# An adaLN + attention + mixture-of-experts layer on one core: second sequence's rows multiplied in the warm-up, three modulation sums in one PSUM bank, partial logits transposed and summed on VectorE

## The chip, the cores and the metric

One Trainium2 chip, and of it one core. The core has TensorE (PE, matrix products; its weight loads are listed apart as PEld), VectorE (DVE), ScalarE (ACT), GpSimd (POOL) and SyncE (SP, which starts most transfers). All work on tiles of up to 128 partitions in on-chip memory; products land in PSUM, in banks of 128 x 512 floats. The metric is the device time of one execution in microseconds, and a verdict compares medians.

## The reference

Everything is float32. Two sequences (B = 2) of 1024 rows with D = 512 go through an adaLN block: attention of a simple kind, then a mixture of eight experts with two chosen per row, and a shared expert.

```
mod = (_silu(L0_c) @ L0_wmod).reshape(B, 6, 1, -1)
sa, ca, ga, sb, cb, gb = mod[:, 0] ... mod[:, 5]
ga, gb = (2 * (g >= 0) - 1) * max(|g|, 0.25)     for g in ga, gb
h = _layernorm(x) * (1 + ca) + sa
Xn = _layernorm(h, gamma, beta)
Q, K, V = split(Xn @ W_in + b_in);  K, V rotated in their first 256 columns
A = 0.5 * sum over rows (cos_sim(K) * cos_sim(V)) + 0.5
x = x + ga * ((A * Q) @ W_out + b_out + h)
h = _layernorm(x) * (1 + cb) + sb
scores = softmax(h @ gate_w);  the 2 best of 8 experts by row
x = x + gb * (sum of w_e * expert_e(h) + shared(h))
```

A depends on all rows of a sequence, so a sequence's K and V come before any of its outputs.

## The kernel before, in words

The 2048 rows are 16 tiles of 128 rows, in four groups of four; tiles 0 to 7 are the first sequence. The program is one instruction stream written out by hand; a scheduler of the tile framework then orders each engine's instructions by what they wait for and by the order in the code. So an instruction that is taken out can change the order of its neighbours. The order inside an engine's queue is fixed when the kernel is built, and an instruction waits for all ahead of it.

*Modulation.* `silu(c)` is turned into a padded operand `sc_pad` of 32 columns for each quarter k of the 512 inputs. `mod_parts` (L235) multiplies, for one of the six parts m, four quarters of the weights side by side: `tile_position=(0, k * CT)` puts quarter k in columns 32k (CT = 32), so four partial sums lie at partitions 0, 32, 64 and 96 of one bank (L240), and ScalarE copies them out (L248). Two forms then add the four partial sums. `spread_now` (L283) multiplies by a selector, `pick`, broadcast to 128 columns: the result has a modulation row copied into all 128 partitions, ready for elementwise use, and ScalarE adds 1 or 0 while copying (L289). `mod_sum` (L250) multiplies by `pick` with its two columns, which gives the two sequences' rows in partitions 0 and 1; `mod_add` adds a constant and stores the row to `mods` in memory, and `mod_gate` forms the clipped gate. The rows are later read back from `mods` into all partitions (`spread`, in `before_mix`), and `turn_mod` transposes two of them on TensorE.

*Start.* `turn_over(n, row)` (L213) multiplies a matrix of ones n times; nobody reads the result. It fills TensorE while data come in: three such products at the start, four after the rows of the first sequence (`ca1[0]`, `sa[0]`). Meanwhile VectorE and ScalarE normalize tiles 0 and 1 (`norm1_in`, `norm1_mid`, `norm1_out`: two layer norms; the outcome is `hn`), and `turn1` transposes a tile (`tr_a`, L330) and lets ScalarE scale it into `xnT` (L377).

*The loop over tiles 0 to 7 of the first sequence.* For tile t: normalize tile t+2, multiply K (`kv_half(t, 0)`: four 128x512 products, L394), transpose tile t+1, do what the table `side` has for t, multiply V (`kv_half(t, 1)`), and accumulate A (`kv_back`). `side` holds the modulation work that isn't needed at once: the second sequence's rows at t = 0, products for ga, cb, sb and gb from t = 1 on, their sums a tile later. Products take turns in three PSUM banks (`mm_ps`), transpositions in others (`tr_ps`).

*The loop over the first sequence's second part, with the second sequence's K and V between.* For tile t: `project` (L555), `norm2` (layer norm again; `hr`), `turn2` (transposition `tr_c`, scaled into `hT` at L586). The table `plan` puts in the second sequence's `kv_half`, `turn1` and `norm1`, the shared expert's chunks (L824, with the sigmoid at L797), and, for each group of four tiles, the routing: `logit_parts` (L624) multiplies four quarters of `gate_w` side by side like the modulation, which leaves partial logits `lgp`, transposed, at partitions 32k + e of a 128 x 512 tile. `route` (L636) multiplies each of the four 128-column pieces by `pick_e`, a 0/1 matrix of 8 columns that sums over k, which also transposes: rows become partitions. VectorE copies the 128 x 32 logits out and goes on with softmax (ScalarE, L654), the two best (L664 and on) and counts; `place_rows` (L689, L692) ranks the rows among those of the same expert, and GpSimd scatters them to `hbuf`. ScalarE loads a table of constants whenever the kind of function changes (square root, exponential, sigmoid).

*After that* the second sequence is projected, the last two groups are routed, and the expert blocks of 128 rows follow (L1416, L1428, L1444, from about 330 us to 640 us), with weights streaming in, and at the end the shared expert's remaining parts and the sums.

Of the kernel before, what the change touches and what calls it, by code (L numbers as in the profile page):

```python
# [8 lines left out]
FP = mybir.dt.float32  # L9
# [3 lines left out]
ALU = mybir.AluOpType  # L13
AX = mybir.AxisListType
# [4 lines left out]
P = 128  # L19
# [5 lines left out]
def kernel(  # L25
# [20 lines left out]
    nc = tc.nc  # L46
    B, S, D = x.shape
    E, _, H = w_gate.shape
    KC = D // P
    CT = P // KC  # L50
# [29 lines left out]
    const = ctx.enter_context(tc.tile_pool(name="const", bufs=1))  # L80
# [16 lines left out]
    def mm_ps(name):  # L97
        return ps_mm.tile([P, 512], FP, tag="mm", name=name)

    def tr_ps(name):  # L100
        return ps_tr.tile([P, 512], FP, tag="tr", name=name)
# [9 lines left out]
    ident = const.tile([P, P], FP, name="ident")  # L111
# [3 lines left out]
    ones_t = const.tile([P, P], FP, name="ones_t")  # L115
# [39 lines left out]
    def load_mod(m, home):  # L155
        t = act_tile(home, f"wmod{m}")
        nc.sync.dma_start(t, wm[:, :, m * D : (m + 1) * D])
        return t
# [32 lines left out]
    wm_ga = load_mod(2, 3)  # L191
# [4 lines left out]
    wm_cb = load_mod(4, 4)  # L196
    wm_sb = load_mod(3, 5)
# [6 lines left out]
    wm_gb = load_mod(5, 0)  # L204
# [5 lines left out]
    def turn_over(n, row):  # L210
        ps = tr_ps(f"turn_over_{n}")
        for _ in range(n):
            nc.tensor.matmul(ps, ones_t, row, start=True, stop=True)  # L213
# [8 lines left out]
    silu = nc.vector.tensor_mul(sc_pad[:, :, 0:B], csb, sig_c)  # L222
    pick = late.tile([P, B], FP, name="pick")
    with tc.issue_after(silu.ins):
        nc.vector.tensor_reduce(
            pick, ident.rearrange("p (k c) -> p c k", k=KC)[:, 0:B, :], AX.X, ALU.add
        )
    pick_e = const.tile([P, E], FP, name="pick_e")
    with tc.issue_after(silu.ins):
        nc.vector.tensor_reduce(  # L230
            pick_e, ident.rearrange("p (k c) -> p c k", k=KC)[:, 0:E, :], AX.X, ALU.add
        )
    parts = {}

    copied = []  # L235
# [11 lines left out]
            )  # L247
        copied.append(nc.scalar.copy(t, ps))  # L248

    def mod_sum(m, w):  # L250
        ps = mm_ps(f"modsum_{m}")
        nc.tensor.matmul(ps[:B, :], pick, w[:, 0, :], start=True, stop=True)
        return ps[:B, :]


    def mod_add(m, w, plus):
        t = w[:B, 1, :]
        nc.vector.tensor_scalar(t, mod_sum(m, w), plus, None, ALU.add)
        nc.sync.dma_start(mods[m], t)
        return t  # L260

    def mod_gate(m, w):

        ps = mod_sum(m, w)
        t, mag = w[:B, 1, :], w[:B, 2, :]
        nc.vector.tensor_scalar(t, ps, 0.0, 2.0, ALU.is_ge, ALU.mult)
        nc.scalar.activation(mag, ps, AF.Abs)
        nc.vector.tensor_scalar(mag, mag, 0.25, None, ALU.max)
        nc.vector.scalar_tensor_tensor(t, t, 1.0, mag, ALU.subtract, ALU.mult)
        nc.sync.dma_start(mods[m], t)  # L270
# [9 lines left out]
        mod_parts(m, w, t)  # L280
        return t

    def spread_now(t, b, plus, tag):  # L283
        ps = mm_ps(f"{tag}_{b}")
        nc.tensor.matmul(
            ps, pick[:, b : b + 1].to_broadcast([P, P]), t, start=True, stop=True
        )
        row = late.tile([P, D], FP, tag=tag, bufs=B, name=f"{tag}_{b}")
        nc.scalar.activation(row, ps, AF.Identity, bias=plus)  # L289
        return row  # L290

    modT = late.tile([P, 2, KC, B], FP, name="modT")

    def turn_mod(i, raw):
        ps = tr_ps(f"modT_{i}")
        for f in range(KC):
            nc.tensor.transpose(
                ps[:, f * B : (f + 1) * B], raw[:, f * P : (f + 1) * P], ident[0:B, 0:B]
            )
        nc.vector.tensor_copy(modT[:, i].rearrange("p f b -> p (f b)"), ps[:, 0 : KC * B])  # L300

    ca1, sa, ga, cb1, sb, gb, cg, sg = ([None] * B for _ in range(8))
    zero_t = const.tile([P, 1], FP, name="zero_t")
# [23 lines left out]
    def transposes(src, name):  # L327
        ps = tr_ps(f"tr_{name}")
        for f in range(KC):
            nc.tensor.transpose(  # L330
                ps[:, f * P : (f + 1) * P], src[:, f * P : (f + 1) * P], ident
            )
        return ps
# [4 lines left out]
    if NS != 4 or B != 2:  # L338
        raise ValueError("the homes are laid out for two sequences of two groups")

    hn_of = {}

    h_of = {}

# [14 lines left out]
    def norm1_out(t):  # L359
        h, b = h_of.pop(t), t // NJ  # L360
        nc.vector.scalar_tensor_tensor(h, h, rs1[:, t : t + 1], sa[b], ALU.mult, ALU.add)
        hn_of[t] = ln.tile([P, D], FP, tag="hn", name=f"hn_{t}")
        normalize(hn_of[t], h, f"b{t}")
# [6 lines left out]
    def turn1(t):  # L370
        g, j = t // 4, t % 4
        hn = hn_of.pop(t)
        if j == 0:
            xnT[g] = act_tile(XNT_HOME[g], f"xnT_{g}")
        ps = transposes(hn, f"a{t}")
        for f in range(KC):
            nc.scalar.activation(  # L377
                xnT[g][:, f, j * P : (j + 1) * P],
                ps[:, f * P : (f + 1) * P],
                AF.Identity,  # L380
                bias=colsb[:, 1, f : f + 1],
                scale=colsb[:, 0, f : f + 1],
            )
# [219 lines left out]
    rows = const.tile([P, NT, TOPK], I32, name="rows")  # L603
# [32 lines left out]
    def route(g, lgp):  # L636

        t0 = g * 4
        ps = tr_ps(f"lg_{g}")
        for j in range(4):  # L640
            nc.tensor.matmul(
                ps[:, j * E : (j + 1) * E],
                lgp[:, j * P : (j + 1) * P],
                pick_e,
                start=True,
                stop=True,
            )
        lg = small.tile([P, 4, E], FP, tag="lg", name=f"lgs_{g}")
        nc.vector.tensor_copy(lg.rearrange("p j e -> p (j e)"), ps[:, 0 : 4 * E])
        mx = small.tile([P, 4], FP, tag="mx", name=f"mx_{g}")  # L650
        nc.vector.tensor_reduce(mx, lg, AX.X, ALU.max)
        nc.vector.tensor_sub(lg, lg, mx.unsqueeze(2).to_broadcast([P, 4, E]))
        ex = small.tile([P, 4, E], FP, tag="ex", name=f"ex_{g}")
        nc.scalar.activation(ex, lg, AF.Exp)  # L654
        sm = small.tile([P, 4], FP, tag="sm", name=f"sm_{g}")
        nc.vector.tensor_reduce(sm, ex, AX.X, ALU.add)
        nc.vector.reciprocal(sm, sm)
        p = small.tile([P, 4, E], FP, tag="p", name=f"p_{g}")
        nc.vector.tensor_mul(p, ex, sm.unsqueeze(2).to_broadcast([P, 4, E]))

        top = small.tile([P, 4, 8], FP, tag="top", name=f"top_{g}")
        place = small.tile([P, 4, 8], U32, tag="place", name=f"place_{g}")
        for j in range(4):
            nc.vector.max(top[:, j, :], p[:, j, :])  # L664
            nc.vector.max_index(place[:, j, :], top[:, j, :], p[:, j, :])
        nc.vector.tensor_copy(wts[:, t0 : t0 + 4, :], top[:, :, 0:TOPK])
        no = small.tile([P, 4, TOPK], FP, tag="no", name=f"no_{g}")
        nc.vector.tensor_copy(no, place[:, :, 0:TOPK])
        pick = picks[:, t0 : t0 + 4]
        for s in range(TOPK):  # L670
            nc.vector.tensor_tensor(
                pick[:, :, s, :],
                no[:, :, s : s + 1].to_broadcast([P, 4, E]),
                ex_no.unsqueeze(1).to_broadcast([P, 4, E]),
                ALU.is_equal,
            )
        both = small.tile([P, 4, E], FP, tag="both", name=f"both_{g}")
        nc.vector.tensor_add(both, pick[:, :, 0, :], pick[:, :, 1, :])
        for j in range(4):
            nc.vector.tensor_add(seen[:, t0 + j + 1, :], seen[:, t0 + j, :], both[:, j, :])  # L680
        return both
# [363 lines left out]
        return kvp.tile([P, D + 2 * R2], FP, tag="acc", bufs=1, name=f"acc_{b}")  # L1045

    def second_rows():
        ca1[1] = spread_now(parts_ca, 1, ones_t[:, 0:1], "ca1")
        sa[1] = spread_now(parts_sa, 1, zero_t, "sa")

    def own(m, w):
        mod_parts(m, w, w[:, 0, :])

    raws = {}

    def add(m, w, plus):
        raws[m] = mod_add(m, w, plus)


    side = {  # L1060
        0: [second_rows],
        1: [lambda: own(2, wm_ga)],
        2: [lambda: mod_gate(2, wm_ga), turn_wq],
        3: [lambda: own(4, wm_cb), lambda: own(3, wm_sb)],
        4: [lambda: add(4, wm_cb, 1.0), lambda: add(3, wm_sb, 0.0)],
        5: [lambda: own(5, wm_gb), lambda: turn_mod(0, raws[4])],
        6: [lambda: mod_gate(5, wm_gb), lambda: turn_mod(1, raws[3])],
        7: [lambda: before_mix(0)],
    }
    turn_over(3, ones_row)  # L1070
    parts_ca = own_parts(1, wm_ca)
# [4 lines left out]
    parts_sa = own_parts(0, wm_sa)  # L1076
    norm1_mid(0)
    sa[0] = spread_now(parts_sa, 0, zero_t, "sa")
    turn_over(4, parts_sa)
    norm1_in(2)  # L1080
    norm1_out(0)
    norm1_mid(1)
    turn1(0)
    norm1_out(1)
    acc = start_acc(0)
    for t in range(NJ):
# [472 lines left out]
    sums = list(range(NT))  # L1559
# [106 lines left out]
```

## Time and profile before

| what | value |
|---|---|
| three runs | 776.17, 777.97 and 780.13 us, median 777.97 |
| profiled execution, its own time | 776.02 us |
| its span, first to last instruction | 774.1 us |
| mean granted TensorE clock | 0.997 of full speed |
| records of the 128x8 logit products (L641) | 32, 256 ns in the median |
| records of the 128x512 modulation sums (L252) | 8, 592 ns in the median |
| records of the side-by-side products (L240) | 48, 592 ns in the median |

The profile names a group of instructions by line, engine, operation and tiles, output first. The matmul records are pipelined: the duration of one (592 ns) is longer than the step from one to the next (about 430 ns), so slots are read from the start of one piece of work to the start of the next. A float32 product leaves two records. "[1.04 <-ACT hn L325]" says that the engine was idle 1.04 us and that the instruction of ScalarE at L325, writing hn, ended that. ScalarE's timeline around one such place:

```profile
173.93 1.28 ACT L316 ACT_TABLE_LOAD   x1
175.23 0.29 ACT L316 ACTIVATE sd_a<-mv,eps_t 128x1 f32<-128x1 f32 x1
175.43 0.79 ACT L586 ACTIVATE hT<-tr_c,modT 128x128 f32<-128x128 f32 x2
178.78 0.29 ACT L316 ACTIVATE sd_b<-mv_b,eps_t 128x1 f32<-128x1 f32 x1 [2.55 <-DVE mv_b L314]
178.98 0.79 ACT L586 ACTIVATE hT<-tr_c,modT 128x128 f32<-128x128 f32 x2
179.66 0.80 ACT L377 ACTIVATE xnT<-tr_a,colsb 128x128 f32<-128x128 f32 x2
```

ScalarE loads the square-root table, then stands idle for 2.55 us with two copies and an xnT queued behind sd_b, until VectorE has delivered mv_b.

### The profile page before, as it was taken

Reading aid. Unit: us, or ns where it says so; the run is one execution under the profiler, and the core shown is the slowest. Engines: PE = TensorE matmul, PEld = TensorE weight load, DVE = VectorE, ACT = ScalarE, POOL = GpSimd, SP = SyncE. Lnnn points to the kernel's source line nnn. Section 1 sums busy time; section 2 is a strip of 40 time slices with the busy share of each in tenths; the row PEclk is TensorE's granted clock in tenths of the full one; section 3 lists DMA queues with packets and bytes.
Section 4 is the critical chain, followed back from the end, with each engine's and each line's share of the span. In section 5 each row is a group of like instructions: output and inputs, shape, how many; then the busy total and the mean of one; then the engine's idle time right before and its main releaser. Section 6 shows DMA issues by size and latency. Waiting matters only on the chain. (4 is left out here: it accounts for less than half of the span.)

```text
span 774.1 us, 8523 instructions
## 1 busy us (share of the span) xinstructions
PE 753.7 (97%) x2547; PEld 418.0 (54%) x2547; DVE 430.1 (56%) x980; ACT 232.0 (30%) x495; POOL 213.4 (28%) x241
## 2 busy tenths in 40 slices
PE   7999999998999999999999999999999999899997
PEld 2444444444444444585566565665656655788542
DVE  4888856898736888893222222322222221499964
ACT  4565513566623054110122111222111221122310
POOL 1234325754622686564100000000000000234530
PEclk9999999999999999999999999999999999999999
DMA  9950002311524811266999999999999975624551
GB/s 322 383 165 29 1 1 73 117 55 45 161 66 161 315 64 42 92 247 220 358 360 364 340 334 327 342 332 338 316 340 340 325 253 193 191 83 134 166 163 54
DMA packets 96368, 158.91 MB, mean 205 GB/s; under 512 B 8088, under 2 KB 51096, under 8 KB 96320
## 3 DMA queue, kind: packets, MB, share of 16 engines
q1 hardware_dynamic: 89984, 138.41, 52.5%
q0 software_dynamic: 5760, 18.88, 7.4%
q10 hardware_dynamic: 576, 1.05, 0.4%
q8 instruction: 22, 0.36, 0.2%
q14 instruction: 26, 0.21, 0.1%
HBM read 128.15 MB, written 30.16 MB: 205 GB/s over the span
## 5 line engine op out<-in xcount | busy, mean ns | idle before, releaser
L1318 POOL DMA_INDIRECT y<-ybuf,yrows x32 | 37.0, 1157 | 334.4 <-SPq L1544 286.7
L394 PE MATMUL kv<-w_kv,xnT 128*128 128x512 f32 x256 | 116.4, 602 | 3.3 <-ACT xnT L377 3.3
L1444 PE MATMUL by<-wd_r,gtT 128*128 128x512 f32 (+1 forms) x210 | 96.1, 593 | 0.9 <-DVEq L1536 0.9
L1416 PE MATMUL bg<-wg_r,hbT 128*128 128x352 f32 x280 | 88.9, 460 | 0.9 <-ACT y L1448 0.9
L1416 PE MATMUL bu<-wu_r,hbT 128*128 128x352 f32 x280 | 88.5, 459 | 0.0
L394 PEld LDWEIGHTS kv<-w_kv,xnT 128*128 128x128 f32 x256 | 47.6, 192 | 61.1 <-issue 49.8
L1416 PEld LDWEIGHTS bu<-wu_r,hbT 128*128 128x128 f32 x280 | 53.2, 190 | 29.6
L1431 DVE COPY gtT<-gtr 128x256 f32<-128x256 f32 x35 | 14.9, 425 | 97.0 <-PE gtr L1428 97.0
L1416 PEld LDWEIGHTS bg<-wg_r,hbT 128*128 128x128 f32 x280 | 50.4, 190 | 23.5 <-ACT y L1448 1.3
L555 PE MATMUL o<-wp,xnT 128*128 128x512 f32 x128 | 57.3, 593 | 0.0
L1295 DVE TENSOR_TENSOR sg_b<-sg_b,bg 128x352 f32<-128x352 f32 x35 | 18.2, 521 | 68.8 <-ACT sg_b L1294 68.8
L1444 PEld LDWEIGHTS by<-wd_r,gtT 128*128 128x128 f32 (+1 forms) x210 | 37.2, 191 | 34.6 <-issue 33.5
L1408 ACT COPY hbT<-tr_b 128x512 f32<-128x512 f32 x36 | 21.1, 586 | 101.4 <-PE tr_b L330 101.4
L1296 DVE TENSOR_TENSOR gt<-sg_b,bu 128x352 f32<-128x352 f32 x35 | 18.3, 521 | 47.2 <-PE bu L1416 47.2
L1448 ACT COPY y<-by 128x512 f32<-128x512 f32 x35 | 20.5, 587 | 70.5 <-PE by L1444 50.7
L555 PEld LDWEIGHTS o<-wp,xnT 128*128 128x128 f32 x128 | 23.8, 190 | 28.6 <-issue 27.0
L1294 ACT ACTIVATE sg_b<-bg 128x352 f32<-128x352 f32 x35 | 16.2, 464 | 76.1 <-PE bg L1416 76.1
L424 POOL TENSOR_TENSOR cross<-kv 128x128 f32<-128x128 f32 x16 | 13.2, 824 | 76.9 <-DVE kv L401 51.1
L417 ACT ACTIVATE sq<-kv 128x512 f32<-128x512 f32 x32 | 20.2, 630 | 32.9 <-DVE kv L401 28.7
L514 PE MATMUL wp<-aw,wqT 128*128 128x512 f32 x64 | 28.6, 597 | 0.9 <-DVE aw L495 0.7
L401 DVE TENSOR_TENSOR kv<-kv,b_kv 128x512 f32<-128x512 f32 x32 | 21.9, 683 | 13.1 <-PE kv L394 12.9
L377 ACT ACTIVATE xnT<-tr_a,colsb 128x128 f32<-128x128 f32 x64 | 24.3, 455 | 15.8 <-PE tr_a L330 15.8
(320 smaller groups left out, 1268.3 us busy)
## 6 DMA issues: line engine op xcount, KB each, us to landing
wg_r<-in_w_gate_dram SPq DMA_DIRECT2D x35, 704.0 KB
wu_r<-in_w_up_dram SPq DMA_DIRECT2D x35, 704.0 KB
wd_r<-in_w_down_dram SPq DMA_DIRECT2D x35, 512.0 KB
hb<-hbuf SPq DMA_DIRECT2D x36, 256.0 KB
ybuf<-y SPq DMA_DIRECT2D x31, 256.0 KB
wd_r<-in_w_down_dram SPq DMA_DIRECT2D x35, 192.0 KB
wmod<-in_wmod_dram SPq DMA_DIRECT2D x6, 1024.0 KB
x<-in_x_dram SPq DMA_DIRECT2D x3, 1024.0 KB
```

Of the source, the lines that this page charges most:

```text
L377: nc.scalar.activation(xnT[g][:, f, j * P : (j + 1) * P], ps[:, f * P : (f + 1) * P], AF.Identity, bias=colsb[:, 1, f : f + 1], scale=cols ...
L394: nc.tensor.matmul(ps, xnT[g][:, k, j * P : (j + 1) * P], w_kv[:, i, k, :], start=(k == 0), stop=(k == KC - 1),)
L401: ins = nc.vector.tensor_add(fronts[t][:, i, :], ps, b_kv[:, i * D : (i + 1) * D])
L417: nc.scalar.activation(sq, kv[:, i, :], AF.Square, accum_out=ss[:, i : i + 1])
L514: nc.tensor.matmul(ps, wqT[:, k, f * P : (f + 1) * P], aw[:, k, :], start=(k == 0), stop=(k == KC - 1),)
L555: nc.tensor.matmul(ps, xnT[g][:, k, j * P : (j + 1) * P], wp[:, k, :], start=(k == 0), stop=(k == KC - 1),)
L1296: nc.vector.tensor_mul(dst, sg[:m, :n], pu[:m, :n])
L1318: nc.gpsimd.indirect_dma_start(out=y, out_offset=None, in_=ybuf, in_offset=bass.IndirectOffsetOnAxis(ap=yrows[:, t, s : s + 1], axis=0), b ...
L1408: nc.scalar.copy(hbT.rearrange("p k q -> p (k q)"), ps)
L1416: nc.tensor.matmul(ps[:, :H], hbT[:, k, :], wt[:, k, :], start=(k == 0), stop=(k == KC - 1))
L1444: nc.tensor.matmul(ps, gtT[:m, c, :], w[2][:m, c, :], start=(c == 0), stop=(c == NH - 1))
L1448: nc.scalar.copy(y, ps)
```

## The change

Three things are changed.

1. The second sequence's rows (`ca1[1]`, `sa[1]`) are multiplied before the loop: `turn_over` after the first sequence's rows makes two products instead of four, and the two row products follow it. Their copies on ScalarE are issued after the last copy of `turn1(0)`. `side[0]` becomes empty.
2. `mod_sum` becomes `mod_sums`, which multiplies the sums of several modulation parts by `pick` into one bank, at columns (and so partitions) 0, 32 and 64. The first gate is summed alone at t = 2 as before; cb, sb and gb together at t = 5. For this the product for gb goes from t = 5 to 4, and both `turn_mod` to t = 6.
3. `route` transposes the four pieces of `lgp` by the identity and lets VectorE sum over k from PSUM, instead of multiplying by `pick_e` and copying; `pick_e` is gone.

```diff
-    pick_e = const.tile([P, E], FP, name="pick_e")
-    with tc.issue_after(silu.ins):
-        nc.vector.tensor_reduce(
-            pick_e, ident.rearrange("p (k c) -> p c k", k=KC)[:, 0:E, :], AX.X, ALU.add
-        )
...
-    def mod_sum(m, w):
-        ps = mm_ps(f"modsum_{m}")
-        nc.tensor.matmul(ps[:B, :], pick, w[:, 0, :], start=True, stop=True)
-        return ps[:B, :]
+    def mod_sums(*ws):
+        ps = mm_ps("modsums")
+        sums = []
+        for i, w in enumerate(ws):
+            rows = slice(i * CT, i * CT + B)
+            nc.tensor.matmul(
+                ps[rows, :], pick, w[:, 0, :], start=True, stop=True, tile_position=(0, i * CT)
+            )
+            sums.append(ps[rows, :])
+        return sums
...
-    def spread_now(t, b, plus, tag):
+    def spread_product(t, b, tag):
         ps = mm_ps(f"{tag}_{b}")
         nc.tensor.matmul(
             ps, pick[:, b : b + 1].to_broadcast([P, P]), t, start=True, stop=True
         )
+        return ps
+
+    def spread_copy(ps, b, plus, tag):
         row = late.tile([P, D], FP, tag=tag, bufs=B, name=f"{tag}_{b}")
         nc.scalar.activation(row, ps, AF.Identity, bias=plus)
         return row
...
-        ps = tr_ps(f"lg_{g}")
-        for j in range(4):
-            nc.tensor.matmul(
-                ps[:, j * E : (j + 1) * E],
-                lgp[:, j * P : (j + 1) * P],
-                pick_e,
-                start=True,
-                stop=True,
-            )
+        ps = transposes(lgp, f"lg{g}")
         lg = small.tile([P, 4, E], FP, tag="lg", name=f"lgs_{g}")
-        nc.vector.tensor_copy(lg.rearrange("p j e -> p (j e)"), ps[:, 0 : 4 * E])
+        nc.vector.tensor_reduce(
+            lg,
+            ps.rearrange("p (j k c) -> p j c k", j=4, k=KC)[:, :, 0:E, :],
+            AX.X,
+            ALU.add,
+        )
...
     side = {
-        0: [second_rows],
+        0: [],
         1: [lambda: own(2, wm_ga)],
-        2: [lambda: mod_gate(2, wm_ga), turn_wq],
+        2: [first_gate, turn_wq],
         3: [lambda: own(4, wm_cb), lambda: own(3, wm_sb)],
-        4: [lambda: add(4, wm_cb, 1.0), lambda: add(3, wm_sb, 0.0)],
-        5: [lambda: own(5, wm_gb), lambda: turn_mod(0, raws[4])],
-        6: [lambda: mod_gate(5, wm_gb), lambda: turn_mod(1, raws[3])],
+        4: [lambda: own(5, wm_gb)],
+        5: [other_sums],
+        6: [lambda: turn_mod(0, raws[4]), lambda: turn_mod(1, raws[3])],
         7: [lambda: before_mix(0)],
     }
...
-    turn_over(4, parts_sa)
+    turn_over(2, parts_sa)
+    rows_1 = second_rows()
     norm1_in(2)
     norm1_out(0)
     norm1_mid(1)
     turn1(0)
+    with tc.issue_after(turned1[0].ins):
+        ca1[1] = spread_copy(rows_1[0], 1, ones_t[:, 0:1], "ca1")
+        sa[1] = spread_copy(rows_1[1], 1, zero_t, "sa")
```

Here `first_gate` and `other_sums` call `mod_sums` and hand its pieces to `mod_add` and `mod_gate`, which no longer sum by themselves; `second_rows` now returns the two products, and `turned1[t]` is the last copy of `turn1(t)`.

More of the change, by code (lines that the diff above doesn't have):

```diff
@@ L248, in mod_parts, with mod_add, mod_gate @@
         copied.append(nc.scalar.copy(t, ps))
-    def mod_sum(m, w):
-        ps = mm_ps(f"modsum_{m}")
-        nc.tensor.matmul(ps[:B, :], pick, w[:, 0, :], start=True, stop=True)
-        return ps[:B, :]
-    def mod_add(m, w, plus):
+    def mod_sums(*ws):
[8 more added lines that the diff above has]
+        return sums
+    def mod_add(m, w, ps, plus):
         t = w[:B, 1, :]
-        nc.vector.tensor_scalar(t, mod_sum(m, w), plus, None, ALU.add)
+        nc.vector.tensor_scalar(t, ps, plus, None, ALU.add)
         nc.sync.dma_start(mods[m], t)
         return t
-    def mod_gate(m, w):
-        ps = mod_sum(m, w)
+    def mod_gate(m, w, ps):
         t, mag = w[:B, 1, :], w[:B, 2, :]
@@ L290, in spread_now @@
         return row
+    def spread_now(t, b, plus, tag):
+        return spread_copy(spread_product(t, b, tag), b, plus, tag)
     modT = late.tile([P, 2, KC, B], FP, name="modT")
@@ L339 @@
         raise ValueError("the homes are laid out for two sequences of two groups")
-    hn_of = {}
+    hn_of, turned1 = {}, {}
     h_of = {}
@@ L376, in turn1 @@
         for f in range(KC):
-            nc.scalar.activation(
+            turned1[t] = nc.scalar.activation(
                 xnT[g][:, f, j * P : (j + 1) * P],
@@ L1047, in second_rows @@
     def second_rows():
-        ca1[1] = spread_now(parts_ca, 1, ones_t[:, 0:1], "ca1")
-        sa[1] = spread_now(parts_sa, 1, zero_t, "sa")
+        return (
+            spread_product(parts_ca, 1, "ca1"),
+            spread_product(parts_sa, 1, "sa"),
+        )
     def own(m, w):
@@ L1054, with first_gate, other_sums @@
     raws = {}
-    def add(m, w, plus):
-        raws[m] = mod_add(m, w, plus)
+    def first_gate():
+        mod_gate(2, wm_ga, *mod_sums(wm_ga))
+    def other_sums():
+        ws = (wm_cb, wm_sb, wm_gb)
+        cb, sb_, gb_ = mod_sums(*ws)
+        raws[4] = mod_add(4, wm_cb, cb, 1.0)
+        raws[3] = mod_add(3, wm_sb, sb_, 0.0)
+        mod_gate(5, wm_gb, gb_)
     side = {
-        0: [second_rows],
+        0: [],
         1: [lambda: own(2, wm_ga)],
-        2: [lambda: mod_gate(2, wm_ga), turn_wq],
+        2: [first_gate, turn_wq],
         3: [lambda: own(4, wm_cb), lambda: own(3, wm_sb)],
-        4: [lambda: add(4, wm_cb, 1.0), lambda: add(3, wm_sb, 0.0)],
-        5: [lambda: own(5, wm_gb), lambda: turn_mod(0, raws[4])],
-        6: [lambda: mod_gate(5, wm_gb), lambda: turn_mod(1, raws[3])],
+        4: [lambda: own(5, wm_gb)],
+        5: [other_sums],
+        6: [lambda: turn_mod(0, raws[4]), lambda: turn_mod(1, raws[3])],
         7: [lambda: before_mix(0)],
```

## The prediction

> **What bounds the kernel now.** I read the page first, for the busiest engine and the chain that ended last.
>
> ```profile
> span 774.1 us, 8523 instructions
> PE 753.7 (97%) x2547; PEld 418.0 (54%) x2547; DVE 430.1 (56%) x980; ACT 232.0 (30%) x495; POOL 213.4 (28%) x241
> PE 14%; DVE 0%; issue 0%
> ```
>
> TensorE works in 753.7 of 774.1 us, so a matmul taken away should shorten the span by its slot, unless TensorE then waits for something else. An average can't say where that happens; the table of busy time by stretch can (stretch, then PE, PEld, DVE, ACT, POOL, granted clock, DMA).
>
> ```profile
> 30.00:60.00 30.00, 29.99 (x111) 13.35 (x110) 26.94 (x63) 17.93 (x47) 12.72 (x17) 1.00 0.64 219
> 160.00:206.00 46.00, 43.25 (x136) 20.98 (x135) 39.54 (x100) 28.54 (x60) 23.37 (x24) 0.96 0.28 86
> 330.00:600.00 270.00, 269.74 (x975) 165.29 (x975) 82.58 (x195) 50.18 (x94) 22.87 (x21) 1.00 0.96 326
> ```
>
> Between 30 and 60 us TensorE is full, but VectorE has only 3.06 of 30 us left. Between 160 and 206 TensorE isn't full and its clock is 0.96. The expert blocks are TensorE-bound and the change doesn't touch them. The list of TensorE's waits says who was late:
>
> ```profile
> PE kv L394 <- ACT xnT L377: 3.3, 2, 2.8
> PE tr_a L330 <- ACT hn L325: 1.0, 1, 1.0
> ```
>
> One wait of 2.8 us dominates. TensorE's timeline (start, length, operation) has it, and the places that the change edits:
>
> ```profile
> 6.67 1.07 PE L240 MATMUL mod<-wmod,sc_pad 128*32 128x512 f32 x8 [0.31 <-DMA wmod<-in_wmod_dram]
> ...
> 12.78 3.60 PE L213 MATMUL turn_over<-parts,ones_t 128*128 128x512 f32 x8
> 17.41 0.66 PE L330 MATMUL tr_a<-ident,hn 128*128 128x128 f32 x4 [1.04 <-ACT hn L325]
> ...
> 22.59 1.02 PE L285 MATMUL ca<-parts,pick 128*128 128x512 f32 x2
> 23.45 1.02 PE L285 MATMUL sa<-parts,pick 128*128 128x512 f32 x2
> 24.30 1.88 PE L394 MATMUL kv<-w_kv,xnT 128*128 128x512 f32 x4
> ...
> 163.03 0.60 PE L330 MATMUL tr_c<-ident,hr 128*128 128x128 f32 x4
> 163.46 0.96 PE L641 MATMUL lg<-pick_e,lgps 128*128 128x8 f32 x8
> 164.27 1.96 PE L824 MATMUL p<-hT,cg 128*128 128x512 f32 x4
> ...
> 175.53 1.88 PE L824 MATMUL p<-hT,cg 128*128 128x512 f32 x4
> 180.17 5.09 PE L394 MATMUL kv<-w_kv,xnT 128*128 128x512 f32 x8 [2.75 <-ACT xnT L377]
> 185.46 3.68 PE L394 MATMUL kv<-w_kv,xnT 128*128 128x512 f32 x8
> ```
>
> A 128x512 fp32 product leaves two records and takes a slot of 0.86 us (22.59 to 23.45). Lengths overlap, so I count from start to start.
>
> **Part 1, the second sequence's rows.** Two products leave the loop: 24.30 − 22.59 = 1.71 us. In the warm-up they replace two of the four products of ones, so that slot stays 3.60, and the 1.04 us wait for hn behind it absorbs any difference. What is moved are the two copies on ScalarE (24.17 and 24.74, 0.57 apart). They now stand behind the transposed tile 0, which ended at 19.60, and ahead of tile 1's hn. ScalarE had 0.36 us idle there, so of 1.14 us some 0.77 pushes hn of tile 1 to 22.3. The build puts one kv product ahead of its transposition, which hides that. VectorE's tile-2 row waits for that buffer (h, one buffer), and behind it stand the kv addition and the first scaling of cs (1.21 us). Replayed with the durations of before, hn of tile 2 ends near 29.8 while TensorE, 1.71 earlier, wants it at 29.47 (31.17 before). Cost 0.35, bounds 0 (if cs slips behind) and 0.77 (the whole push). Net −1.36.
>
> **Part 2, modulation sums.** Four 2x512 sums of one slot each, 4 x 0.86 = 3.44. After: the first gate alone, 0.86, and three in one slot at columns 0, 32 and 64. No row shows 2-column weights side by side. The nearest is L240: eight records of four column groups in 1.07 us, 1.00 from 31.70 to the next kv at 32.70. So 0.86 + 1.00 = 1.86, a gain of 1.58. Bounds: 0 gain if they run one by one (4 x 0.86 again), 1.72 if three cost 0.86. I take the L240 row, whose positions are the same. The products and additions that move between tiles 4, 5 and 6 cost TensorE nothing new. Tile 5 gets about 3.1 us of VectorE work in one lump, behind which the normalizing of the next tile queues. Its cover is the earlier hn (hn of tile 3 ended a tile ahead of use); without it the lump less the slack of 3.06 per 30 us would show, up to 1 us. I take 0. The stores to mods and the loads of the rows are queued on SP in another order, but their readers come after 97 us, and the DMA share falls to 0.06 at 60 to 90 us. On SP and POOL the loads of again and cu and the scatters to hbuf also change places; the blocks that read hbuf begin after 320 us, so 100 us cover them, and a late row would be paid at that point in full.
>
> [...]
>
> **Part 3, logits.** Per group four L641 products cost 164.27 − 163.46 = 0.81; four transpositions cost 163.46 − 163.03 = 0.43. Four groups: 4 x 0.38 = 1.52 off TensorE. VectorE's copy (0.19) becomes a reduction of 128x128 to 128x32. Nearest: 0.20 (128x8 from 128x32) and 0.28 (128x8 from 128x128, L756). I take 0.28, bounds 0.19 and 0.69 (a statistics pass over 512). That is +0.1 each, against 0.38 earlier start: the logits come 0.28 sooner. The reduction building pick_e (0.2) goes. Net −1.52, bounds −1.52 and +0.5 (4 x (0.69 − 0.19 − 0.38), where the next work waits for the logits). Group 1's route now ends with a load of the square-root table more, 1.28 us near 205 where ScalarE is idle a third of the time; uncovered it would delay nrm, and so one accumulation, not a product.
>
> **The wait at 177.** Everything changed shifts the scheduler's choice there. Before, ScalarE's queue is exp, square-root table, sd_c, sigmoid table, sg, hr, square-root table, hT, sd_b, hT, xnT. Built after, sd_c precedes exp, one table load (1.28) goes, but hr precedes the sigmoid table, and hn of tile 13 and all four hT precede the first xnT. Replay: hr from 171.4 (off_c waits for VectorE's 1.69 us row), table, sg 173.4 to 174.0, VectorE sg 174.25, gT, h 175.85 to 177.1, mv_b 177.9, off_b 178.8, hn 178.9 to 179.7, four hT (0.40 each) to 181.1, xnT, kv at 181.5. TensorE is ready at 177.25 (rank, now ahead of kv, in that): a wait of 4.2 instead of 2.75, +1.45. Bounds: 0 wait (−2.75) if the queue runs otherwise, 7.5 if an item of VectorE's (39.5 of 46 us busy) goes ahead too.
>
> The clock adds to it. After 2.75 us of idling, kv took 5.09 for what took 3.68 at full rate: 1.41 lost; the granted clock in 180 to 182 us is 0.50. The halved stretch is 3.4 us in the trace, so a wait that covers its start fully costs up to 3.4/2 = 1.7: +0.29. Bounds: −1.41 without a drop, +1.7 for a second stretch. Together +1.74.
>
> [...]
>
> **Sum.** −1.71 + 0.35 − 1.58 − 1.52 + 1.74 = −2.7 us. The profiled execution took 776.02 us, 1.92 beyond its span; it lies 1.95 below the median, 777.97. Span 771.4, execution 773.3, median 775.3.
>
> **Rivals.**
> - *The wait shrinks or goes.* For it: one table load less, and mv_b directly behind st_b on VectorE (u stood between: 0.65). Against: four hT and a hn ahead of xnT. If gone with its clock loss (2.75 + 1.41): −4.46 − 4.16 = −8.6, 769.4; halved, 771.4.
> - *Sums run one after the other* (weights of 2 columns are another form than L240's 32). Part 2 gives 0: −1.1, 776.9. Against: the same column positions as L240.
> - *Slower: the wait at 177 grows.* VectorE is 86% busy there and decides when sd_b can run; each item ahead of it is 0.7 to 1.3, each table load 1.28. With a wait of 7.5 and both stretches slow (1.4 + 1.7): 10.6 against 4.16, +6.4 − 4.46 = +2.0, 780.0. It decides the sign from a wait plus clock loss of 8.6. A second such wait in the loop (VectorE 90% busy) at 4.2 more would give 784.
>
> **How the numbers follow.** Forecast 0.45; wait shrinks 0.25; sums in turn 0.12; slower 0.18. The likeliest's own range, from its bounds on parts 1 and 3 and 0.7 us on the wait, is 773.5 to 777. Eight in ten needs the shrunken wait and half of the slower case: 769.4 to 780.5. What this measurement tells from no change is 0.5%, 3.9 us: faster is below 774.1, slower above 781.9. Faster: all of the 0.25 and a third of the forecast, 0.40. Slower: over half of the slower case, 0.12. Same: 0.48.
>
> **What would show it.** Part 1: no L285 product between tile 1's transposition and kv, a hn wait near 29 us below 0.8. Part 2: modsums records starting together, next work 1.0 after. Part 3: transposed logits in 0.43 four times, the reduction near 0.28. The wait at about 177: 3.5 to 4.9 us, at half clock after. A gap at 177 under 2, or a new gap over 1 us between 22 and 97, makes the sum wrong.

## The result and the profile after

The changed kernel takes 777.34 us in the median of 14 runs (775.75 to 778.97), the kernel before 777.06 (774.31 to 780.13): a ratio of 1.0004, 95% interval 0.999 to 1.0017. No difference can be seen. The forecast was 2.7 us less.

The profiled execution of the changed kernel is one of its long ones, 778.63 us. First its page.

```profile
span 776.8 us, 8477 instructions
PE 754.8 (97%) x2527; PEld 417.3 (54%) x2527; DVE 428.7 (55%) x979; ACT 232.6 (30%) x495; POOL 215.0 (28%) x241
```

TensorE has less to do and is busy 1.1 us longer: some of its instructions ran more slowly. TensorE's waits (us in all, times, longest):

```profile
PE rank L693 <- ACT hT L593: 3.9, 1, 3.9
...
PE amix L465 <- DVE acc L462: 1.3, 1, 1.3
...
PE wqT L488 <- ACT xnT L384: 0.5, 1, 0.5
PE wqT L488 <- ACT wqT L491: 0.3, 1, 0.3
```

The wait at 177 us is 3.9 instead of 2.8, and of another product (rank). The waits before amix (the products that sum the first sequence's A over its rows) and wqT are new; the kernel before had none there. Its lines at amix, VectorE's last step ahead of it, TensorE, and the busy times of one slice (granted clock third from the right):

```profile
96.84 0.28 DVE L455 TENSOR_TENSOR acc<-half 128x128 f32<-128x128 f32 x1
97.52 0.95 PE L458 MATMUL amix<-ones_t,acc 128*128 128x1 f32 x8
...
106.84 1.02 PE L524 MATMUL row<-rowp,ones_t 128*128 128x512 f32 x2
```

```profile
100.00:102.00 2.00, 1.73 (x5) 0.68 (x4) 1.96 (x5) 2.00 (x7) 1.22 (x3) 1.00 0.00 0
```

The timeline of the changed kernel shows the edited places and what follows the waits:

```profile
29.77 0.66 PE L337 MATMUL tr_a<-ident,hn 128*128 128x128 f32 x4
...
68.17 1.03 PE L251 MATMUL modsums<-wmod,pick 128*2 128x512 f32 x6
69.13 7.13 PE L401 MATMUL kv<-w_kv,xnT 128*128 128x512 f32 x16
...
97.11 1.05 PE L465 MATMUL amix<-ones_t,acc 128*128 128x1 f32 x8 [1.30 <-DVE acc L462]
98.03 0.64 PE L337 MATMUL tr_a<-ident,hn 128*128 128x128 f32 x4
99.06 8.83 PE L521 MATMUL wp<-aw,wqT 128*128 128x512 f32 x16 [0.40 <-DVE aw L502]
107.73 1.02 PE L531 MATMUL row<-rowp,ones_t 128*128 128x512 f32 x2
...
164.35 0.60 PE L337 MATMUL tr_lg<-ident,lgps 128*128 128x128 f32 x4
164.78 3.60 PE L828 MATMUL p<-hT,cg 128*128 128x512 f32 x8
...
181.71 0.63 PE L693 MATMUL rank<-both,before_t 128*128 128x32 f32 x2 [3.87 <-ACT hT L593]
...
182.59 9.80 PE L401 MATMUL kv<-w_kv,xnT 128*128 128x512 f32 x16
192.22 0.60 PE L337 MATMUL tr_c<-ident,hr 128*128 128x128 f32 x4
```

Sixteen records of 128x512 take 7.1 us in the loop (69.13), 8.83 behind amix and 9.80 behind the wait at 177. The busy times by stretch say why (the third number from the right is the granted clock):

```profile
98.00:100.00 2.00, 1.60 (x8) 0.76 (x7) 1.80 (x6) 1.30 (x4) 1.23 (x3) 0.82 0.00 0
100.00:102.00 2.00, 2.00 (x4) 0.96 (x3) 1.97 (x5) 2.00 (x6) 1.57 (x2) 0.50 0.00 0
102.00:104.00 2.00, 2.00 (x5) 0.81 (x4) 1.39 (x3) 0.13 (x1) 0.06 (x1) 0.83 0.00 0
...
182.00:188.00 6.00, 6.00 (x11) 2.90 (x11) 3.91 (x15) 2.35 (x7) 2.43 (x2) 0.50 0.11 44
```

The clock is halved for about 3.4 us from 99.3 to 102.7 (0.36 + 1.00 + 0.34 of full speed lost in three slices of 2 us: 1.7 us), and for twice that up to 188. In the kernel before it is 1.00 from 96 to 108.

So the ledger of landmarks, before to after, in us: tile 2's transposition 31.17 to 29.77 (−1.40); tile 4's 50.05 to 49.78 (−0.27, the waits at wqT took 1.1); tile 8's 86.34 to 84.47 (−1.87, the sums added 1.6); amix 97.52 to 97.11 (−0.41, the wait of 1.30); the row product 106.84 to 107.73 (+0.89, the clock); the first group's p 164.27 to 164.78 (+0.51, the logits); the end of tile 12's kv 188.97 to 192.22 (+3.25, the wait and the clock); the first ph of the blocks 319.67 to 320.80 (+1.13, three more groups' logits and shorter waits behind them); the end +2.7, of which 1.7 come from a half clock near 663 that this execution has (0.62 and 0.53 in the slices from 662 to 666), behind a wait of 2.0 us that both kernels have, and that the profiled execution of before doesn't (1.00 there).

### The profile page after: what moved, and what is told of

Its sections match the earlier page's. It is cut to its first block, busy times and chain, and to the rows that moved or that the text cites. A ratio compares the mean times of both kernels' runs of the same rounds, so it can differ in the third digit from the quotient of the medians.

```text
span 776.8 us, 8477 instructions
## 1 busy us (share of the span) xinstructions
PE 754.8 (97%) x2527; PEld 417.3 (54%) x2527; DVE 428.7 (55%) x979; ACT 232.6 (30%) x495; POOL 215.0 (28%) x241
```

## The experiments

Theory A: what the parts take off TensorE is real, but before 97 us and at 177 us VectorE's queue decides when the next operand is ready, so TensorE waits instead of working, and behind the waits its clock halves. Theory B: every part is worth its slots; only the reordering at 177 loses.

**The three parts alone, and two together.** Each kernel is the one before with one part of the change as its diff shows it (the rows: lines of `second_rows`, `turn_over(2, ...)` and the copies behind `turned1[0]`; the sums: `mod_sums` and the table `side`; the logits: `route`).

```diff
only_rows, on before
...
-    turn_over(4, parts_sa)
+    turn_over(2, parts_sa)
+    rows_1 = second_rows()
...
only_sums, on before
...
-        4: [lambda: add(4, wm_cb, 1.0), lambda: add(3, wm_sb, 0.0)],
...
+        4: [lambda: own(5, wm_gb)],
+        5: [other_sums],
...
only_logits, on before
...
+        ps = transposes(lgp, f"lg{g}")
...
+        nc.vector.tensor_reduce(
...
```

> The second sequence's rows in the warm-up alone, the sums and the logits as before. Theory A (the work taken off TensorE before 97 us is returned where VectorE's queue ends the first sequence's sum): the transposition of tile 2 comes near 29.8 instead of 31.17, TensorE's wait before amix grows from 0 to 0.5 or more, amix starts at 97.0 to 97.5 (97.52 before), the wait at 177 stays near 2.75, and the whole is within 1.5 us of before. Theory B (each part is worth the slot that it removes, and only the reordering at 177 loses): amix near 96.1 and the whole 1.4 us faster, ratio 0.998.

> The three modulation sums side by side alone, the rest as before. Theory A: transposition of tile 8 near 84.8 (86.34 before), amix still at 97.0 to 97.5, the whole within 1.5 us of before. Theory B: amix near 95.9, the whole 1.6 us faster, ratio 0.998. Both: the three sums take one slot, next work 0.95 to 1.0 after their start.

> Both modulation parts, the logits as before; ScalarE's and TensorE's order at 177 is that of before. Theory A: TensorE waits 1 us or more before amix, which starts near 97, and the clock may halve behind it; the whole 0 to 1.5 us slower or at best 0.5 faster. Theory B: 2.9 us faster, ratio 0.996; the wait at 177 stays at 2.75.

> Logits transposed and summed on VectorE alone, the modulation as before. The order at 177 is that of the changed kernel (rank ahead of kv, all four hT ahead of xnT). Theory A and B: wait at 177 of 3.5 to 4.2 instead of 2.75 with half clock behind it, second kv product ends 2.5 to 3.5 later than before; two later groups return 0.75. The whole 0.5 to 2.5 us slower. Rival (the reordering costs nothing by itself, the longer wait comes from TensorE being early): wait 2.75 to 3.2 and the whole 1 us faster.

Measured, ratios to the kernel before on the same chip: only_rows 1.0027 (1.0013 to 1.004), slower; only_sums 0.9999 (0.9986 to 1.0012); rows_and_sums 1.0 (0.9987 to 1.0014); only_logits 0.9996 (0.9984 to 1.0009). The timeline of only_rows around amix:

```profile
98.64 1.05 PE L464 MATMUL amix<-ones_t,acc 128*128 128x1 f32 x8 [1.21 <-DVE acc L461]
...
100.59 9.02 PE L520 MATMUL wp<-aw,wqT 128*128 128x512 f32 x16 [0.40 <-DVE aw L501]
109.45 1.02 PE L530 MATMUL row<-rowp,ones_t 128*128 128x512 f32 x2
```

Tile 2's transposition came at 29.80, as expected, and yet amix came 1.1 us later than before: VectorE ends its last step ahead of it at 98.58 instead of 97.12, the wait is 1.21, and the clock halves (0.84, 0.50 and 0.81 in the slices from 100 to 106). VectorE loses most of that between 72 and 80 us, where it waits 1.70 us for ScalarE's hn (0.19 before). This is more than theory A had asked for (97.0 to 97.5), and theory B falls for the rows.

In the profiled executions of only_sums and only_logits the first kv product took 5.40 us for 3.70 (granted clock 0.86 over 18 to 30 us in only_sums, 1.00 in before), so that their landmarks stand 1.8 us late. With that taken off, amix is at 97.5 in only_logits, as before, and at 96.8 in only_sums: the sums alone bring it 0.7 us of their 1.6 earlier, between theory A (97.0 to 97.5) and theory B (95.9). The wait there is 0.61, and the clock stays full behind it (1.00 in every slice from 96 to 110). rows_and_sums has amix at 96.97, a wait of 1.29, and the clock halves (0.89, 0.50 and 0.75 in the slices from 98 to 104); against only_rows (98.64) the sums bring it 1.67 earlier. So it is the rows that make VectorE late. In only_logits the wait at 177 is that of the changed kernel,

```profile
PE rank L681 <- ACT hT L581: 3.9, 1, 3.9
```

so part 3 alone moves rank and hT. But it is not 0.5 to 2.5 us slower as I had expected: the three later groups' logits, and waits behind them that shrink (rank for both, 0.9 us before, is gone), give back what the longer wait costs. Its profiled execution also lost one stretch of half clock behind the wait (kv in 8.81 us; 0.86, 0.50 and 0.78 in the slices from 182 to 188), where the changed kernel lost two (9.80). That expectation was a miss.

**Work without use, to hold the clock.** Two products of ones go ahead of amix in the changed kernel; nobody reads them.

```diff
fill_amix, on after
+    fill_ps = mm_ps("fill")
+    for _ in range(2):
+        nc.tensor.matmul(fill_ps, ones_t, fronts[NJ][:, 0, :], start=True, stop=True)
     aT = mix(0, acc)
     norm1(NJ + 2)
```

> The changed kernel with two products of ones (1.72 us, nobody reads them) put on TensorE ahead of amix, in the 1.3 us that it waits there. Clock theory (the change's gain is lost because TensorE's new pauses halve its clock behind them): amix starts near 97.5 instead of 97.1, but the clock stays at 1.00 from 98 to 104 and the row product starts at 106.3 to 106.9 instead of 107.7; the mean granted clock of the runs rises from 0.9917 by 0.001 to 0.002 and the whole is 0.5 to 1.5 us faster than the changed kernel, with more work on TensorE. Rival (the waits alone cost the time, the clock is chance): row near 108.1 and the whole 0.4 us slower than the changed kernel.

Measured: 774.61 us, 0.997 of before (0.9956 to 0.9985). The timeline and one slice of it (granted clock third from the right):

```profile
95.39 1.88 PE L1130 MATMUL fill<-kv,ones_t 128*128 128x512 f32 x4
97.10 0.95 PE L465 MATMUL amix<-ones_t,acc 128*128 128x1 f32 x8
...
99.29 7.13 PE L521 MATMUL wp<-aw,wqT 128*128 128x512 f32 x16 [0.74 <-DVE aw L502]
106.26 1.02 PE L531 MATMUL row<-rowp,ones_t 128*128 128x512 f32 x2
```

```profile
100.00:102.00 2.00, 2.00 (x6) 0.80 (x6) 1.93 (x5) 1.46 (x5) 0.81 (x2) 1.00 0.00 0
```

amix is where it was, wp takes 7.13 instead of 8.83, and the row product comes 1.5 us earlier. The mean granted clock of the runs rises from 0.9917 to 0.9954. The clock theory holds; the rival asked for a slower kernel. The gain (2.7 us between medians, 2.0 between means) is more than the 0.5 to 1.5 expected. The rise of the clock is more than one stretch of half clock accounts for (1.7 of 775 us, 0.0022); what of the gain comes from other places than this one is open.

**VectorE's order ahead of amix.** Three us of tile 10's normalizing stood ahead of the first sequence's sum. They now come behind `mixed`, the last subtraction of `mix`.

```diff
pin_norm, on after
...
-    norm1(NJ + 2)
+    with tc.issue_after(mixed[0].ins):
+        norm1(NJ + 2)
...
pin_and_fill, on pin_norm, in mix behind the four amix products
+        if b == 0:
+            fill_ps = mm_ps("fill")
+            nc.tensor.matmul(fill_ps, ones_t, acc[:, 0:D], start=True, stop=True)
```

> The changed kernel with the normalizing of tile 10 held on VectorE and ScalarE behind the last step of the first sequence's sum; before, 3 us of it stood ahead of that step. If VectorE's order decides amix: wait before amix 0 to 0.4, amix at 95.8 to 96.2, no half clock behind it, row at 105 to 105.7, the whole 2 to 3 us faster than the changed kernel (ratio to before 0.996 to 0.998). If the chain over GpSimd decides instead: amix stays within 0.4 of 97.1 and the time within 1 us.

> The changed kernel with tile 10's normalizing behind the first sequence's sum and one product of ones (0.86 us, nobody reads it) between amix and wp, where TensorE then waits 1.19 us. Clock theory: clock 1.00 from 96 to 106, row at 104.8 to 105.2 instead of 106.4 with the pin alone, mean granted clock of the runs up by 0.001 to 0.002, the whole 1 to 1.5 us faster than with the pin alone and 3 us faster than the changed kernel. Rival (waits alone count): row at 106.4, no gain over the pin alone.

The timeline of pin_norm:

```profile
95.60 0.95 PE L467 MATMUL amix<-ones_t,acc 128*128 128x1 f32 x8
97.74 8.83 PE L523 MATMUL wp<-aw,wqT 128*128 128x512 f32 x16 [1.19 <-DVE aw L504]
106.41 1.02 PE L533 MATMUL row<-rowp,ones_t 128*128 128x512 f32 x2
```

amix starts at 95.60 without a wait, so VectorE's order did decide it. But TensorE then waits 1.19 us for wp's operand, wp takes 8.83 with the clock halved (0.56 and 0.58 in the slices from 98 to 102), which was not expected, and the row product comes at 106.41: the gain of 1.5 us at amix is 1.3 at the row, and not the 2 to 2.7 expected. The time is 776.9 us, 0.9977 (0.9959 to 0.9995): the ratio is the expected one, but the runs spread from 772.8 us at a mean clock of 0.997 to 777.85 at 0.990. With one product of ones in the new pause:

```profile
96.73 0.95 PE L467 MATMUL amix<-ones_t,acc 128*128 128x1 f32 x8
97.54 1.11 PE L476 MATMUL fill<-acc,ones_t 128*128 128x512 f32 x2
98.86 7.13 PE L526 MATMUL wp<-aw,wqT 128*128 128x512 f32 x16 [0.22 <-DVE aw L507]
105.83 1.02 PE L536 MATMUL row<-rowp,ones_t 128*128 128x512 f32 x2
```

The clock stays full (1.00 in every slice from 94 to 110). (This execution had lost 1.7 us behind 18 us, where the first kv took 6.26 us against 4.56 with the pin alone: the transposition of tile 1 is at 24.82 against 23.11 with the pin alone; from amix to the row product it is 9.10 us against 10.81.) 774.01 us, 0.9963 (0.995 to 0.9977): the fastest version of the study, 3.1 us below the kernel before. The pin and the fill were not tried on the kernel before; its amix has no wait to take away.

**The wait at 177.** The second shared chunk's other six products go ahead of tile 12's kv, in both kernels.

```diff
chunk_ahead, on after; chunk_ahead_before, on before
-        7: [(turn2, 6), (turn1, T + 4), (kv_half, T + 4, 0), (ranks, 0)],
+        7: [(turn2, 6), (turn1, T + 4), (chunk, 1), (kv_half, T + 4, 0), (ranks, 0)],
...
-        (chunk, 1),
         (kv_half, T + 5, 0),
```

> The changed kernel with the second shared chunk's remaining products (six of 0.86 us) ahead of tile 12's kv on TensorE, where it waits 3.87 us. If that wait and the half clock behind it are what takes the gain: no wait over 1 us near 177, clock 1.00 from 176 to 192, and the whole 5 to 6.5 us faster than the changed kernel (771 to 773). If the time is only moved to a later wait: a new wait of 2 us or more between 190 and 240 and less than 2 us gained.

> The same move in the kernel before, whose wait there is 2.75 us with 1.4 us of half clock behind it: 3 to 4.2 us faster than before (ratio 0.995 to 0.996). With the move the changed kernel then stands 1.5 to 3 us ahead of this one if the three parts are worth what they take off TensorE, and level with it if they are not.

chunk_ahead 0.9984 (0.9971 to 0.9997), chunk_ahead_before 0.9991 (0.9977 to 1.0005): far less than the gain expected of either. The wait has moved, which was the expectation's second alternative:

```profile
188.79 0.60 PE L337 MATMUL tr_c<-ident,hr 128*128 128x128 f32 x4
193.07 1.12 PE L337 MATMUL tr_a<-ident,hn 128*128 128x128 f32 x4 [3.68 <-DVE rk L704]
```

The transposition waits for the bank of rank, which VectorE reads at 192.83, behind 18 us of other work in which it idles 1.7 us. The kernel before with the same move resumes at 193.12: there the two kernels are level, 0.05 us apart. I then put rank behind that transposition, first with the fill of two products, then with the pin and one.

```diff
fill_chunk_late_ranks, on chunk_ahead with the fill; all_edits, on chunk_ahead with pin and fill
-        7: [..., (chunk, 1), (kv_half, T + 4, 0), (ranks, 0)],
+        7: [..., (chunk, 1), (kv_half, T + 4, 0)],
...
         (turn1, T + 5),
+        (ranks, 0),
```

> The changed kernel with the two products of ones ahead of amix, the second chunk's products ahead of tile 12's kv, and group 0's ranks behind the transposition of tile 13, so that this transposition no longer waits for VectorE to read the rank's bank (3.68 us with the chunk moved alone). If that bank is what holds TensorE: no wait above 1 us between 170 and 240, clock 1.00 there, logits of group 1 near 201 instead of 204.8, the whole 3 us or more faster than with the fill alone (769 to 772). If VectorE's amount of work holds it: a new wait of 2 us or more between 189 and 250 behind another product, and less than 1.5 us gained.

> The same, with the pin and one product of ones behind amix in place of two ahead of it. 1 to 1.5 us faster than fill_chunk_late_ranks if TensorE is the bound from 96 to 240, within 0.5 us of it if VectorE is.

0.9996 (0.9984 to 1.0008) and 0.997 (0.9955 to 0.9985). The wait is 3.73 us again, now at 191 us, before rank, for hT, and the clock halves behind it (0.52, 0.50, 0.50 and 0.77 in the slices from 194 to 202, in all_edits 0.88, 0.50, 0.50, 0.50 and 0.91 from 192 to 202). So the first is no gain over the fill alone (0.997), as the second alternative of its expectation had it. The second expectation failed both ways: all_edits is 1.9 us faster than fill_chunk_late_ranks, more than either alternative. Wherever the work is put, TensorE of the changed kernel stands 3 to 4 us between 170 and 200 us. I read that as the amount of VectorE's and ScalarE's work there; no run takes any of that work away.

**The clock at 177.** On pin_and_fill, the gate half of the second chunk (four products instead of two) and two products of ones stand in that wait. `h_last[t]` is tile t's h as `norm1_out` leaves it.

```diff
fill_177, on pin_and_fill
-        7: [(turn2, 6), (turn1, T + 4), (kv_half, T + 4, 0), (ranks, 0)],
+        7: [(turn2, 6), (turn1, T + 4), (half_chunk, 1), (fill, T + 5, 2), (kv_half, T + 4, 0), (ranks, 0)],
...
+    def fill(t, n):
+        ps = mm_ps(f"fill_{t}")
+        for _ in range(n):
+            nc.tensor.matmul(ps, ones_t, h_last[t], start=True, stop=True)
...
```

> pin_and_fill with TensorE kept at work through the wait at 177 as well: the second chunk's gate half (four products instead of two) and two products of ones stand ahead of tile 12's kv. Clock theory: clock 1.00 from 174 to 190, both kv products of tile 12 in 6.9 to 7.1 us instead of 9.8, tile 13's transposition at 188 to 189 instead of 191.3, and unless VectorE is the bound right behind, the whole 2 to 4 us faster than pin_and_fill (770 to 772, ratio 0.991 to 0.994). If VectorE's amount of work holds the stretch: a new wait of 1.5 to 4 us between 185 and 240 and less than 1 us gained.

```profile
179.26 3.70 PE L402 MATMUL kv<-w_kv,xnT 128*128 128x512 f32 x8 [0.79 <-ACT xnT L385]
...
187.93 0.65 PE L337 MATMUL tr_a<-ident,hn 128*128 128x128 f32 x4 [0.66 <-DVE rk L710]
...
202.48 0.66 PE L337 MATMUL tr_lg<-ident,lgps 128*128 128x128 f32 x4 [2.40 <-ACT lgps L646]
```

The clock part holds: 1.00 from 176 to 194, both halves of kv in 3.7 us each, the transposition at 187.93, the mean clock of the runs 0.9965. But there is a new wait of 2.40 at 200 us, and the time is 774.96 us, 0.9974 (0.9964 to 0.9985), no better than pin_and_fill. The size of the wait is that of the second alternative, VectorE's amount of work, but its cause is another: ScalarE, which copies lgps out, had stood 6.51 us behind a single VectorE product (the last section has it).

```profile
199.20 0.29 ACT L323 ACTIVATE sd_b<-mv_b,eps_t 128x1 f32<-128x1 f32 x1 [6.51 <-DVE mv_b L321]
```

**All runs by clock.** Each run lists its span and its mean granted clock. A straight line through the runs of a kernel, read at clock 0.995, compares spans at one clock:

| kernel | runs | mean clock | span at 0.995, us |
|---|---|---|---|
| before | 116 | 0.9957 | 775.8 |
| after | 14 | 0.9917 | 773.3 |
| only_rows | 12 | 0.9937 | 776.4 |
| only_sums | 12 | 0.9952 | 775.2 |
| rows_and_sums | 12 | 0.9948 | 775.1 |
| only_logits | 12 | 0.9942 | 774.2 |
| fill_amix | 12 | 0.9954 | 773.7 |
| pin_norm | 12 | 0.9927 | 772.4 |
| pin_and_fill | 12 | 0.9947 | 772.4 |
| chunk_ahead | 12 | 0.9942 | 773.7 |
| chunk_ahead_before | 12 | 0.9969 | 775.8 |
| fill_chunk_late_ranks | 12 | 0.9937 | 774.0 |
| all_edits | 12 | 0.9943 | 772.7 |
| fill_177 | 12 | 0.9965 | 774.4 |

At one clock the changed kernel is 2.5 us shorter (read at the upper end of its own clocks, 0.990 to 0.995). A clock lower by 0.001 costs 0.6 us (the slope of every line is 540 to 670 us for 1.0), and its runs have 0.0040 less: 2.4 us, which takes the gain back. The line alone is a correlation; that the clock is the cause was shown at one place, between amix and the row product, by fill_amix and by pin_and_fill against pin_norm, whose spans at one clock are the same.

The table also divides the gain. The runs of before come from four chips, which taken alone give 775.5 to 776.0, so a few tenths of a us say little; in brackets, the difference from the runs on the same chip. At one clock the logits alone are 1.6 us shorter than before (1.3), near the 1.52 that they take off TensorE. The sums alone are 0.6 shorter (0.3), the rows alone 0.6 longer (0.9), both together 0.7 shorter (0.4), where 2.94 was forecast. With the chunk moved in both kernels, the changed one is 0.4 us ahead in the median and 2.1 at one clock. fill_177 is the reverse of the changed kernel: it has a high clock, but at one clock it is 2.0 us longer than pin_and_fill.

## Why the prediction was wrong on the sum

The time lies inside the range, and "within 0.5%" had the highest chance, but the forecast of 2.7 us less did not come: that the time lies inside is the width of the range, and no merit of the sum. The prediction's own sign for a wrong sum, a new gap over 1 us between 22 and 97, did come: the 1.30 before amix.

- *Part 1*: tile 2's transposition was to come 1.36 us earlier and came 1.40 earlier. The step that failed is the one behind it: I let the 1.36 run through to the end. 1.1 went into waits at wqT, and alone the part is slower (1.0027; 0.6 to 0.9 us at one clock), for VectorE's queue, with 3.06 of 30 us to spare by my own table, ended its last step before amix 1.46 us later. I had not looked at amix in the profile of before, where VectorE ended that step at 97.12 and TensorE came at 97.52: a cover of 0.4 us.
- *Part 2*: three sums in a slot of 0.96 us (1.00 expected), gain as computed on TensorE. The term for tile 5's lump of VectorE work, taken as 0, was too small where the sums stand alone: of 1.6 us, 0.7 arrived at amix, so 0.9 was lost, inside my bound of 1 us. Behind the rows nothing more was lost (98.64 to 96.97).
- *Part 3*: transposition 0.43 and reduction 0.28 us (275 to 292 ns in four), both as expected, and 1.3 to 1.6 us at one clock for the 1.52 of the sum.
- *The wait at 177*: 3.87 for 4.2, with the queue order as replayed (sg at 173.5, off_b at 179.2). But it is rank that waits, for a bank of the two that hold transpositions, which the last hT frees; I had counted rank as work before the wait. The clock behind it was mis-sized: two stretches of 3.4 us, not one, about 2.8 us lost (9.80 against 7.0) where I took 1.7. The second stretch stood in my bounds. What of this reaches the end is not separated by any run.
- *The clock elsewhere* is the term that was missing. I charged the clock only to the wait that had it before, and not to the 1.3 us wait that could appear before amix, behind which 1.7 us were lost. Over all runs the mean clock fell by 0.0040, worth 2.4 us.

Behind waits of much the same length the clock halved in one place and not in another. Behind 1.30 + 0.40 us of waiting in the changed kernel, with only amix and a transposition between, it halved (0.82, 0.50 and 0.83 in the slices from 98 to 104), and so it did in pin_norm behind 1.19 us with amix alone ahead of it (0.56 and 0.58 from 98 to 102). Behind 0.61 + 0.40 us in only_sums it stayed at 1.00, and behind 1.27 + 0.40 us at the same place in the profile of chunk_ahead too (1.00 from 90 to 112, the row product at 106.38). Of two waits near 18 us that are almost the same, 1.15 + 0.55 us left it full in the changed kernel's profile (1.00 over 18 to 30 us, the first kv in 4.56 us), and behind 1.18 + 0.55 us the same ten records took 6.26 us in that of pin_and_fill. No run here shows what separates these cases.

## What to carry to other kernels

On an engine that is 97% busy, a slot taken away is a gain only as far as the next operand comes earlier too; look at the slack of every such hand-over on the way to the next barrier, here 0.4 us at amix. Then ask what the new pause does to TensorE's clock: here pauses of 1.2 and 1.3 us, in the profiles of pin_norm and of the changed kernel, each had some 1.7 us of lost clock behind them, and two products that nobody reads made the kernel faster (774.61 us for 777.34). Compare versions by their mean granted clock as well as by their time.

## What the runs showed of the hardware

*The half clock comes in stretches of about 3.4 us, and not in every execution.* Summed over slices of 2 us, the loss behind amix is 1.7 us, behind 177 in the changed kernel 3.4, near 662 1.7. The wait of 2.0 us before 662 is in all kernels; the profiled executions of before and of chunk_ahead_before kept their clock there (1.00) and those of the others did not (0.50 to 0.56 in their slowest slice of 2 us). The same wait of 2.75 us at 177 had one stretch behind it in only_rows (kv in 5.40 us; 0.82, 0.50 and 0.83 from 182 to 188) and none in only_sums (3.70; 1.00). The runs of before lie between 0.993 and 1.0 in mean clock. What starts a stretch, no run here shows.

*Single VectorE products took several us while GpSimd worked without a gap.* In fill_177, one VectorE product of 128x512 took 7.07 us where others take 0.68. VectorE's line, and then four of GpSimd's seven of the same time:

```profile
191.27 7.07 DVE L427 TENSOR_TENSOR pr<-kv 128x512 f32<-128x512 f32 x1
```

```profile
191.49 1.29 POOL L607 TENSOR_TENSOR hr<-hr,cb 128x512 f32<-128x512 f32 x1
192.72 1.27 POOL L1055 TENSOR_TENSOR ca<-ca,ga 128x512 f32<-128x512 f32 x1
...
196.12 1.26 POOL L1056 TENSOR_TENSOR sa<-b_o,sa 128x512 f32<-128x512 f32 x1
197.34 0.44 POOL L434 TENSOR_TENSOR dsum<-cross 128x128 f32<-128x128 f32 x1
```

GpSimd has its seven operations directly one behind the other from 191.49 to 197.8, and VectorE's product ends at 198.34, 0.6 us behind them. The new wait of 2.40 in fill_177 comes some 4 us later, and the trace links them: mv_b stands behind this product on VectorE, ScalarE waited 6.51 us for mv_b (the line above), and the copy lgps, for which TensorE waits, stands behind that on ScalarE. No run takes the product away. In the kernel before the same product took 2.23 us. In pin_and_fill a product of 128x1, which takes 0.21 us at 163.28, shows the same:

```profile
198.64 3.15 DVE L443 TENSOR_TENSOR w<-inv 128x1 f32<-128x1 f32 x1
```

It ends at 201.79, and GpSimd works there without a gap from 195.66 to 201.77. That GpSimd's operations are what held these products up is read from these times alone; no run took the two apart.
